# A graph layer's edge kernel: one-hots against PSUM constants, the node picked on VectorE, last edges found in blocks

## The chip, the cores and the metric

The kernel runs on one core of a Trainium2 chip. The core has five engines with queues of their own: TensorE (PE in the profile, its weight loads PEld), VectorE (DVE), ScalarE (ACT), GpSimd (POOL) and SyncE (SP, which here only issues DMAs). Each runs its instructions in the order in which they stand, and engines wait for each other by semaphores. The metric is the device time of one execution in microseconds.

## The reference

A graph with 12,500 nodes of 32 features and 400,000 edges, sorted by the node they end in (dst). Nodes are normalised and clipped, each edge gets a two-layer perceptron of its source row, its end's row and its own 32 features, and each node takes the largest result of its edges:

```python
h = jnp.maximum(_layernorm(x, axis=-1), 0.0)
rol, col = src, dst                              # edges, sorted by dst
e_feat = jnp.concatenate([h[rol], h[col], edge_attr], axis=-1)
hid = jax.nn.relu(e_feat @ W1 + b1)              # 96 -> 64
v = hid @ W2 + b2                                # 64 -> 32
x_cand = jax.ops.segment_max(v, col, num_segments=num_nodes)
return x + jnp.maximum(x_cand, h)
```

## The kernel before

**Layout.** The edges are cut into four stripes (NS = 4) that lie on four groups of 32 partitions, and each stripe into 196 chunks of C = 512 edges. Edges are handled a chunk at a time (2,048 edges over all stripes), two chunks c and c+1 per turn of the main loop, 98 turns in all. Node p * 98 + t lies in partition p, column t. Those 98 columns are also read as 7 groups (A1) of 14 (A0).

**Where a source row comes from.** A chunk needs 16 blocks of 128 source rows. Twelve of them are fetched by GpSimd with indirect DMAs from the copy of h in DRAM (`gather`, L148: one instruction per block of 128 rows, three to a buffer, 24 buffers). The other four (MM = 4) are made by TensorE, in what the code calls a tile (`tile(c, m)`, L344 to L359): h stands in SBUF as two float32r parts (`hs`, the rounded value and the rest), a one-hot over (partition, group) picks for each of 128 edges the group of 14 nodes that holds its source, and 7 groups x 2 parts = 14 matmuls with the one-hot as weights and `hs` as moving data (L356) add up to a 128 x 448 result: 14 candidate nodes x 32 features per edge. A matmul in front of these (L353) adds -1e30 to all candidates but one: its weights are `its`, a bfloat16 one-hot of the edge's place within its group, its moving data the constant table `others`. So a maximum over the 14 (L359, VectorE, out of PSUM) is the node's row.

**One-hots.** They are made by VectorE, chunk by chunk: seven tensor_scalar compares of the key row `kb` (float16, broadcast to all partitions by DMA) with the partition's own number (L340), and an eighth for `its` (L342). `kb` holds two rows per chunk, key and place.

**A turn of the loop** (L476 to L533), with a = c + 2 and b = c + 3, is written out by hand, and each engine keeps that order. GpSimd gathers for a and b. TensorE: tile (a,0); the first layer's source part (L444 with ht); tiles (a,1) and (a,2); the first layer's edge part for a and b (L444 with ea); the second layer for c and c+1 (L506) into two `pv` buffers, which are the same two that the tiles use; the first layer's end part (L444 with of and qw); the one-before-last chunk's reduction (L430); tile (a,3); transposes (L420); tile (b,0); L430; tile (b,1); L420; tiles (b,2) and (b,3). VectorE takes each tile's maximum, turns gathered rows into features with 32 x 32 transposes (`to_features`, L400 and L403), makes the one-hots of b and a + 2, scans each chunk along its edges (L513, a running maximum that restarts at each new node), adds the bias (L422) and makes `last` (L410), which marks each node's last edge within a window of 32 nodes, from `at`. ScalarE applies the first layer's relu (L491), makes the end's one-hot `of` with a square and a relu (L386, L387) and copies out results (L434), which SP writes to two tables `top_d` with one DMA per stripe. SP also loads ea and the window rows qw; db, pb and kb are issued from ScalarE's queue.

**Before the loop** x is normalised (VectorE for three of the four pieces, GpSimd for the piece with index GP = 3, L171 to L207), h is written to DRAM (L207), keys are computed and written, a penalty `pen` per edge is made from dst (L233, L234), h is split into its two parts (L241, L242) and q = h W1 for the end's part is computed (L249 to L267). Then a stage of its own (L271 to L303) loads all of dst, the next dst and the windows' limits and computes `at`, 196 chunks x 4 stripes at once, and a flag `general` that says whether the input breaks the assumptions of the fast path. These stages and the loop use pools that take over each other's memory, so a later one starts when the earlier one is done with it.

**After the loop** the two tables are read back (L546, L547) and merged (L549); h is put together again by GpSimd as the sum of its two parts (L541); maximum with h, sum with x, and out (L627 to L629).

The functions that the change touches follow with their line numbers.

Of the kernel before, what the change touches and what calls it, by code (L numbers as in the profile page):

```python
# [46 lines left out]
AHEAD = 4  # L47
PIECE = 2 * A0
GP = 3
ROUND = 12582912.0  # L50
LOW = 1e30
ZERO = 784
# [9 lines left out]
def gnn_kernel(ctx, tc, x, src, src_mm, src_t, dst, dst_next, dst_ext, lo, lo_c, hi, edge_attr, weights, w1, w2, b2, out):  # L62
# [19 lines left out]

# [9 lines left out]
    key_d = dram.tile([2, len(MMC) * MM * P], F16, name="key_d")  # L92
# [7 lines left out]
    for k, r in enumerate(pieces):  # L100
        (nc.sync, nc.scalar)[k % 2].dma_start(xs[:, r], x_v[:, r])
# [7 lines left out]
    iota_w = const.tile([P, W], F32, name="iota_w")  # L109
    nc.gpsimd.iota(iota_w, pattern=[[1, W]], base=0, channel_multiplier=0,  # L110
                   allow_small_or_imprecise_dtypes=True)
    below = const.tile([P, NCH], F32, name="below")
    for s in range(NS):
# [3 lines left out]
    place = const.tile([P, 1], F32, name="place")  # L117
    nc.gpsimd.iota(place, pattern=[[0, 1]], base=0, channel_multiplier=1,
                   allow_small_or_imprecise_dtypes=True)
    key_p = const.tile([P, A1], F32, name="key_p")  # L120
    nc.gpsimd.iota(key_p, pattern=[[1, A1]], base=0, channel_multiplier=A1,
                   allow_small_or_imprecise_dtypes=True)
    hs = const.tile([P, 2, A1, D, A0], F32R, name="hs")
    others = const.tile([P, D, A0], BF16, name="others")
# [13 lines left out]
    at = const.tile([P, NS, TS], F32, name="at")  # L138
# [14 lines left out]

    with tc.tile_pool(name="nodes", bufs=1) as pool, tc.tile_pool(name="nodes_ps", bufs=2, space=PSUM) as ps:
        zero = pool.tile([P, ZERO], F32, name="zero")
# [3 lines left out]
        sts = [pool.tile([P, 2, PIECE], F32, name=f"st{k}") for k in range(len(pieces))]  # L159
        shares = [(nc.vector, st, r) for st, r in zip(sts, pieces)]  # L160
        shares.append((nc.gpsimd, *shares.pop(GP)[1:]))
# [3 lines left out]
        iota_a = pool.tile([P, D, A0], F32, name="iota_a")  # L165
        nc.gpsimd.iota(iota_a, pattern=[[0, D], [1, A0]], base=0, channel_multiplier=0,
                       allow_small_or_imprecise_dtypes=True)
        lo_w = pool.tile([P, NCH], I32, name="lo_w")
        nc.scalar.dma_start(lo_w, ap(lo, 0, [[NCH, NS], [0, W], [1, NCH]]))

# [12 lines left out]
        with tc.manual_schedule(engines={DVE, SP}):  # L183
            for v, st, r in shares:
                n = r.stop - r.start
                total(v, st[:, 0, :n], xs[:, r])
                mean = st[:, 0, :n, None].to_broadcast([P, n, D])
                if v is nc.vector:
                    v.scalar_tensor_tensor(h[:, r], mean, -1.0 / D, xs[:, r], op0=ALU.mult, op1=ALU.add)
                else:  # L190
                    v.tensor_scalar(st[:, 0, :n], st[:, 0, :n], 1.0 / D, None, op0=ALU.mult)
                    v.tensor_tensor(h[:, r], xs[:, r], mean, op=ALU.subtract)
                nc.scalar.activation(sq[:, r], h[:, r], AF.Square)
            for v, st, r in shares:
                n = r.stop - r.start
                total(v, st[:, 1, :n], sq[:, r])
                nc.scalar.activation(st[:, 0, :n], st[:, 1, :n], AF.Sqrt, scale=1.0 / D, bias=eps)
            for v, st, r in shares:
                n = r.stop - r.start
                nc.vector.reciprocal(st[:, 1, :n], st[:, 0, :n])  # L200
                factor = st[:, 1, :n, None].to_broadcast([P, n, D])
                if v is nc.vector:
                    v.scalar_tensor_tensor(h[:, r], h[:, r], 0.0, factor, op0=ALU.max, op1=ALU.mult)
                else:
                    v.tensor_scalar(h[:, r], h[:, r], 0.0, None, op0=ALU.max)
                    v.tensor_tensor(h[:, r], h[:, r], factor, op=ALU.mult)
                nc.sync.dma_start(h_v[:, r], h[:, r])  # L207


            def group(out, of):  # L210
                nc.vector.tensor_scalar(out, of, 1.0 / A0, 0.5 / A0 - 0.5, op0=ALU.mult, op1=ALU.add)
                nc.vector.tensor_scalar(out, out, ROUND, None, op0=ALU.add)
                nc.vector.tensor_scalar(out, out, ROUND, None, op0=ALU.subtract)

            sp = pool.tile([P, len(MMC) * MM], I32, name="sp")
            nc.sync.dma_start(sp, src_mm)
            key = pool.tile([P, len(MMC) * MM], F32, name="key")
            group(key, sp)
            key16 = pool.tile([P, 2, len(MMC) * MM], F16, name="key16")
            nc.vector.tensor_copy(key16[:, 0], key)  # L220
            nc.vector.scalar_tensor_tensor(key16[:, 1], key, -float(A0), sp, op0=ALU.mult, op1=ALU.add)
            nc.sync.dma_start(key_d.rearrange("k (p e) -> p k e", p=P), key16)

            nc.vector.tensor_scalar(others, iota_a, place, -LOW, op0=ALU.not_equal, op1=ALU.mult)
            nc.vector.tensor_tensor(below, below, lo_w, op=ALU.subtract)


            de = pool.tile([P, EP // P + 1], I32, name="de")
            nc.sync.dma_start(de, ap(dst_ext, 0, [[EP // P, P], [1, EP // P + 1]]))
            pen = pool.tile([P, EP // P], BF16, name="pen")  # L230
            for k in range(0, EP // P, EP // P // 4):
                r = slice(k, k + EP // P // 4)
                nc.vector.tensor_tensor(pen[:, r], de[:, k + 1:k + 1 + EP // P // 4], de[:, r], op=ALU.not_equal)  # L233
                nc.vector.tensor_scalar(pen[:, r], pen[:, r], -LOW, None, op0=ALU.mult)  # L234
            nc.sync.dma_start(pen_d.rearrange("(p e) -> p e", p=P), pen)

        for r in pieces:
            g = slice(r.start // A0, r.stop // A0)
            h1, h2 = (hs[:, k, g].rearrange("p g f a -> p g a f") for k in range(2))
            hr = h[:, r].rearrange("p (g a) f -> p g a f", a=A0)  # L240
            nc.scalar.activation(h1, hr, AF.Copy)  # L241
            nc.vector.tensor_tensor(h2, hr, h1, op=ALU.subtract)  # L242

        for t in top_d:
            nc.scalar.dma_start(ap(t, 0, [[NT * D, P], [ZERO, NT * D // ZERO], [1, ZERO]]),
                                zero[:, None, :].to_broadcast([P, NT * D // ZERO, ZERO]))


        q_v = q_d.rearrange("(p t) o -> p t o", p=P)  # L249
        qs = pool.tile([P, NT, HID], F32, name="qs")  # L250
        for t in range(0, NT, 16):
            fours = [(k, min(4, NT - k)) for k in range(t, min(t + 16, NT), 4)]
            rows = fours[0][1] * D
            hp = ps.tile([P, 4, P], F32, name="hp")
            for i, (k, n) in enumerate(fours):
                nc.tensor.transpose(hp[:n * D, i], h[:, k:k + n].rearrange("p t f -> p (t f)"), ident)
            ht = pool.tile([P, 4, P], F32, name="ht", bufs=2)
            nc.vector.tensor_copy(ht[:rows, :len(fours)], hp[:rows, :len(fours)])
            for i in range(0, len(fours), 2):
                two = fours[i:i + 2]  # L260
                pp = ps.tile([P, 8, HID], F32, name="pp", bufs=4)
                for j, (k, n) in enumerate(two):
                    nc.tensor.matmul(pp[:, 4 * j:4 * j + n].rearrange("p t o -> p (t o)"), ht[:n * D, i + j],
                                     wq[:n * D, :n * HID], start=True, stop=True)
                k, n = two[0][0], sum(n for _, n in two)
                nc.scalar.activation(qs[:, k:k + n], pp[:, :n], AF.Copy)
        nc.sync.dma_start(q_v, qs)  # L267

    with tc.tile_pool(name="windows", bufs=1) as pool, tc.tile_pool(name="windows_ps", bufs=1, space=PSUM) as ps:  # L271
        lo_b = pool.tile([P, NS, NCH], I32, name="lo_b")
        hi_b = pool.tile([P, NS, NCH], I32, name="hi_b")
        nc.scalar.dma_start(lo_b, ap(lo, 0, [[0, P], [NCH, NS], [1, NCH]]))
        nc.scalar.dma_start(hi_b, ap(hi, 0, [[0, P], [NCH, NS], [1, NCH]]))
        di = pool.tile([P, NS, TS], I32, name="di")
        dn = pool.tile([P, NS, TS], I32, name="dn")
        nc.scalar.dma_start(di.rearrange("p s t -> p (s t)"), dst)
        nc.scalar.dma_start(dn.rearrange("p s t -> p (s t)"), dst_next)
        bad = pool.tile([P, 4, NS], F32, name="bad")  # L280
        step = pool.tile([P, TS], F32, name="step")
        wide = pool.tile([P, NCH], F32, name="wide")
        for s in range(NS):

# [22 lines left out]
    with tc.tile_pool(name="edges", bufs=3) as pool, tc.tile_pool(name="edges_ps", bufs=1, space=PSUM) as ps, \  # L307
# [8 lines left out]
        nc.vector.tensor_copy(iota_ps, iota_w)  # L316
        mm_rows = {}
        gh = {}
        hts = {}

        def load_keys(c):

# [369 lines left out]
```

## Time and profile before

| | us |
|---|---|
| median of 3 runs | 3158.97 (3158.54 to 3159.71) |
| the profiled execution, timed | 3161.57 |
| its span, first to last instruction | 3159.8 |
| TensorE busy | 3038.9 |
| GpSimd busy | 2331.2 |
| VectorE busy | 1822.4 |
| ScalarE busy | 562.8 |
| first gather starts | 31.05 |
| first tile's first matmul | 95.99 |
| last gather starts | 3059.8 |
| mean granted TensorE clock | 0.983 of full speed |

A row of the profile names the line, the engine, the operation, the tiles as out<-in, the count, the time busy in all and the mean of one, and then the idle time of the engine in front of it with what ended it. Matmuls overlap one another, so that the busy time of one is longer than the distance from one to the next. In a timeline the first two columns are start and duration in us, and idle time stands in brackets. GpSimd's busy time holds the issuing of a gather, not its transfer.

### The profile page before, as it was taken

To read this page: it belongs to the slowest core of one execution; us is meant where nothing else is said; L and a number is where in the kernel's file an instruction comes from. 1 tells how busy PE (TensorE), PEld (TensorE's weight loads), DVE (VectorE), ACT (ScalarE), POOL (GpSimd) and SP (SyncE) were. 2 spreads that over 40 slices of the span, in tenths; PEclk is the share of its full clock that TensorE was granted. 3 is DMA by queue.
4 is the path that set the end of the run, shared out by engine and by line. 5 is a ranking of instruction groups with operands and counts; after the bars stand their busy time and mean duration, and the time that the engine had idled before them with its cause. 6 is when DMAs were issued, how large, how long until landed. Compare 5 with 4: busy or idle time off the path is not lost. (4 is left out here: it accounts for less than half of the span.)

```text
span 3159.8 us, 59504 instructions
## 1 busy us (share of the span) xinstructions
PE 3038.9 (96%) x21969; PEld 2382.0 (75%) x21969; DVE 1822.4 (58%) x3999; ACT 562.8 (18%) x1007; POOL 2331.2 (74%) x2377
## 2 busy tenths in 40 slices
PE   2799999999999999999999999999999999999995
PEld 1578787777778777777778777777778777777873
DVE  6455555555555555555555555555555555555554
ACT  2121212112121212112121211112121211212121
POOL 7777777777777777777777777777777777777751
PEclk7899999999999999999999999999999999999997
DMA  6323332332333233233323332332333233233321
GB/s 246 109 64 74 90 73 63 90 80 68 72 89 76 64 84 83 71 69 89 78 64 77 88 72 63 90 83 64 73 89 76 64 87 85 66 72 88 78 57 63
DMA packets 203030, 255.38 MB, mean 81 GB/s; under 512 B 116062, under 2 KB 154862, under 8 KB 189551
## 3 DMA queue, kind: packets, MB, share of 16 engines
q10 hardware_dynamic: 42364, 138.10, 14.0%
q1 hardware_dynamic: 85330, 74.88, 10.1%
q0 software_dynamic: 75040, 38.57, 8.8%
q8 instruction: 173, 2.83, 0.4%
q14 instruction: 123, 1.00, 0.1%
HBM read 237.24 MB, written 14.05 MB: 80 GB/s over the span
## 5 line engine op out<-in xcount | busy, mean ns | idle before, releaser
L148 POOL DMA_INDIRECT gh<-h_d,src_i x2345 | 2301.2, 981 | 731.3 <-issue 567.8
L356 PE MATMUL pv<-hs,hot 128*128 128x448 f32 x10920 | 2435.0, 376 | 0.0
L356 PEld LDWEIGHTS pv<-hs,hot 128*128 128x128 f32 x10920 | 2058.5, 189 | 150.2 <-issue 0.3
L359 DVE TENSOR_REDUCE gm<-pv 128x32 f32<-128x448 f32 x780 | 486.3, 623 | 1149.9 <-PE pv L356 1147.7
L340 DVE TENSOR_SCALAR hot<-kb,key_p 128x512 fp32r<-128x512 f16 x1365 | 584.0, 487 | 6.1 <-DMA kb<-key_d 6.1
L491 ACT ACTIVATE hid<-ph,wt 128x512 f32<-128x512 f32 x392 | 237.2, 688 | 1325.7 <-PE ph L444 1312.2
L513 DVE TENSOR_TENSOR_SCAN sm<-pb,sm,pv 128x512 f32<-128x512 bf16 x195 | 249.6, 1280 | 133.4 <-PE pv L506 122.8
L353 PE MATMUL pv<-others,its 128*128 128x448 bf16 x780 | 281.3, 361 | 17.3 <-DMA qw<-q_d 10.6
L434 ACT ACTIVATE wo<-tr 128x64 f32<-128x64 f32 x196 | 43.7, 223 | 1146.6 <-PE tr L430 1056.4
L400 DVE STREAM_TRANSPOSE ht<-gh 128x96 f32<-128x96 f32 x782 | 209.5, 268 | 0.0
L353 PEld LDWEIGHTS <-its 128*128 128x128 bf16 x780 | 74.9, 96 | 172.4 <-issue 151.8
L430 PEld LDWEIGHTS tr<-so,last 128*64 128x64 f32 x3136 | 108.0, 138 | 112.6 <-issue 107.0
L386 ACT ACTIVATE of<-db,below 128x512 f32<-128x512 int32 x196 | 141.4, 721 | 64.5 <-DMA db<-in_dst_ext 64.5
L387 ACT ACTIVATE of<-of,ones 128x512 f32<-128x512 f32 x196 | 142.3, 726 | 6.4
L430 PE MATMUL tr<-so,last 128*64 128x64 f32 x3136 | 135.2, 229 | 3.3 <-DVE so L422 3.3
L410 DVE TENSOR_TENSOR last<-iota_ps,at 128x512 f32<-128x512 f32 x196 | 132.8, 678 | 0.0
L422 DVE TENSOR_TENSOR so<-tr,wt 128x512 f32<-128x512 f32 x196 | 127.9, 653 | 3.0 <-PE tr L420 3.0
L420 PE MATMUL tr<-ident,sm 128*128 128x128 f32 x784 | 117.8, 272 | 1.5 <-DVE sm L513 0.8
L444 PE MATMUL ph<-ht,wt 32*64 32x512 f32 x1568 | 111.3, 617 | 0.0
L420 PEld LDWEIGHTS tr<-ident,sm 128*128 128x128 f32 x784 | 97.4, 141 | 16.7 <-ACT wo L434 2.0
L506 PE MATMUL pv<-hid,wt 64*32 64x512 f32 x1568 | 109.3, 605 | 0.7 <-ACT hid L491 0.7
L444 PE MATMUL ph<-ea,wt 32*64 32x512 f32 x1568 | 109.1, 613 | 0.0
(78 smaller groups left out, 478.4 us busy)
## 6 DMA issues: line engine op xcount, KB each, us to landing
ea<-in_edge_attr SPq DMA_DIRECT2D x49, 1024.0 KB
db<-in_dst_ext ACTq DMA_DIRECT2D x49, 1024.0 KB
kb<-key_d ACTq DMA_DIRECT2D x97, 512.0 KB
gh<-h_d,src_i POOLq DMA_INDIRECT x2345
pb<-pen_d ACTq DMA_DIRECT2D x49, 512.0 KB
qw<-q_d SPq DMA_DIRECT2D x784, 8.0 KB
top_d<-wo SPq DMA_DIRECT2D x784, 4.0 KB
top_d<-zero ACTq DMA_DIRECT2D x2, 1568.0 KB
```

The costliest lines, as they stand in the source:

```text
L148: nc.gpsimd.indirect_dma_start(out=parts[-1][:, i, :], out_offset=None, in_=h_d[:, :], in_offset=bass.IndirectOffsetOnAxis(ap=src_i[:, c, ...
L340: nc.vector.tensor_scalar(hot[:, k], keys[c][:, 0], key_p[:, k:k + 1], None, op0=ALU.is_equal)
L353: nc.tensor.matmul(po, its[:, e], others.rearrange("p f a -> p (f a)"), start=True, stop=False)
L356: nc.tensor.matmul(po, hot[:, k, e], hs[:, part, k].rearrange("p f a -> p (f a)"), start=False, stop=(k == A1 - 1 and part == 1))
L359: nc.vector.tensor_reduce(rows, po.rearrange("p (f a) -> p f a", a=A0), axis=AX.X, op=ALU.max)
L387: nc.scalar.activation(of, of, AF.Relu, bias=ones, scale=-1.0)
L400: nc.vector.transpose(ht[:, r].rearrange("p k e -> p (k e)"), gh[c][part][:, :r.stop - r.start].rearrange("p k f -> p (k f)"))
L420: nc.tensor.transpose(px[:, j, :], sm[:, j * P:(j + 1) * P], ident)
L430: nc.tensor.matmul(pw[g * 2 * W:(g + 1) * 2 * W], last[:, j, 2 * g:2 * g + 2].rearrange("p s w -> p (s w)"), so[:, j, g * 2 * D:(g + 1) * ...
L444: nc.tensor.matmul(ph[s][x * HID:(x + 1) * HID], w[g], e[g], start=start, stop=stop)
L491: nc.scalar.activation(hid[s], ph[s], AF.Relu, bias=b1c)
L513: nc.vector.tensor_tensor_scan(sm, loaded.pop(c + x)[2], pv[x], before, op0=ALU.add, op1=ALU.max)
```

## The change

It has five parts.

1. **The pick.** `its`, `others` and the matmul L353 go; `key_d` and `kb` hold one row per chunk. `tile` multiplies the 128 x 448 result with a mask of the edge's place in its group (`mask_of`, made once per chunk for four tiles) and takes the maximum of the product, which is the node's row since h is not negative. The places are computed on the chip from `src_i` (`places`), for 16 chunks ahead of the loop and for the rest in one turn of it.
2. **The one-hots.** The constants that are compared with (`counts`: places in a window, key numbers, places in a group) lie in PSUM. Five of the seven groups are made by VectorE with two tensor_tensor compares (2 and 3 groups), two by ScalarE with a square and a relu each.
3. **Last edges.** `at` is computed in 14 blocks of 14 chunks, each loaded by four DMAs on ScalarE's queue one turn ahead and computed between two tiles (`load_block`, `make_block`); the stage in front of the loop goes. The flag is put together after the loop.
4. **Memory and order at the start.** What the tiles need has a pool of its own (`early`, `early_ps`) that is there from the start, so that the tiles of chunks 0 and 1 stand among the node stages; the order of all engines but GpSimd is written out by hand from there on. GpSimd's part of the normalisation is shorter: the last product of its piece is VectorE's. The penalty's scaling is ScalarE's, the zero fills of `top_d` are issued by SP.
5. **h at the end** is summed by GpSimd right behind its last gather, into the memory of `src_i`.

```diff
-            for k in groups:
-                nc.vector.tensor_scalar(hot[:, k], keys[c][:, 0], key_p[:, k:k + 1], None, op0=ALU.is_equal)
-            if A1 - 1 in groups:
-                nc.vector.tensor_scalar(its, keys.pop(c)[:, 1], place, None, op0=ALU.is_equal)
+    consts = early_ps.tile([P, C], F32, name="consts")[:, :W + A1 + A0]
+    count_ps, key_ps, place_ps = consts[:, :W], consts[:, W:W + A1], consts[:, W + A1:]
+    nc.vector.tensor_copy(consts, counts)
...
+    def one_hots(c, start, stop):
...
+        nc.vector.tensor_tensor(hot_of(c)[:, start:stop], keys[c][:, None, :].to_broadcast([P, n, MM * P]),
+                                key_ps[:, start:stop, None].to_broadcast([P, n, MM * P]), op=ALU.is_equal)
+    def one_hots_act(c, groups=BY_ACT):
...
+            nc.scalar.activation(away, keys[c], AF.Square, bias=key_n[:, k:k + 1])
+            nc.scalar.activation(hot_of(c)[:, k], away, AF.Relu, bias=ones, scale=-1.0)
+    def mask_of(c):
...
+            nc.vector.tensor_tensor(
+                masks[c], place_ps[:, None, :].to_broadcast([P, MM, A0]),
+                place_k[:, (c - MMC.start) * MM:(c - MMC.start + 1) * MM, None].to_broadcast([P, MM, A0]),
+                op=ALU.is_equal)
```

```diff
-            nc.tensor.matmul(po, its[:, e], others.rearrange("p f a -> p (f a)"), start=True, stop=False)
             for k in range(A1):
                 for part in range(2):
                     nc.tensor.matmul(po, hot[:, k, e], hs[:, part, k].rearrange("p f a -> p (f a)"),
-                                     start=False, stop=(k == A1 - 1 and part == 1))
-            nc.vector.tensor_reduce(rows, po.rearrange("p (f a) -> p f a", a=A0), axis=AX.X, op=ALU.max)
+                                 start=(k == 0 and part == 0), stop=(k == A1 - 1 and part == 1))
+        of_group = po.rearrange("p (f a) -> p f a", a=A0)
+        one = early.tile([P, D, A0], F32, name="one", bufs=2)
+        nc.vector.tensor_tensor(one, of_group, masks[c][:, m, None, :].to_broadcast([P, D, A0]), op=ALU.mult)
+        nc.vector.tensor_reduce(mm_rows[c][:, m, :], one, axis=AX.X, op=ALU.max)
```

```diff
+    def make_block(b):
+        di, dn, lo_b, hi_b = loaded_b.pop(b)
+        at = ats[b] = early.tile([P, NS * BLOCK, J], F32, name="at")
...
+        nc.vector.tensor_tensor(at, di, lo_b[:, :, None].to_broadcast([P, NS * BLOCK, J]), op=ALU.subtract)
+        nc.vector.tensor_tensor(step, di, dn, op=ALU.is_gt)
+        nc.vector.tensor_reduce(bad[:, b, 0:1], step, axis=AX.XY, op=ALU.max)
+        nc.vector.tensor_tensor(step, di, dn, op=ALU.not_equal)
+        nc.vector.scalar_tensor_tensor(at, at, 1.0, step, op0=ALU.add, op1=ALU.mult)
+        nc.vector.tensor_tensor(wide, hi_b, lo_b, op=ALU.subtract)
+        nc.vector.tensor_reduce(bad[:, b, 1:2], wide, axis=AX.X, op=ALU.max)
```

The loop's turn with its new calls, and the end:

```diff
+            if (c + 6) % BLOCK == 0 and (c + 6) // BLOCK < NB:
+                load_block((c + 6) // BLOCK)
+            if a == NCH - 2:
+                nc.gpsimd.tensor_tensor(again.rearrange("p (g a) f -> p g a f", a=A0),
+                                        hs[:, 0].rearrange("p g f a -> p g a f"),
+                                        hs[:, 1].rearrange("p g f a -> p g a f"), op=ALU.add)
             tile(a, 0)
...
-            one_hots(b, range(3))
+            one_hots_act(b)
+            one_hots(b, 0, 2)
             tile(a, 1)
             to_features(a, 1)
-            one_hots(b, range(3, A1))
+            one_hots(b, 2, BY_ACT.start)
+            mask_of(b)
             last = [lasts(c)]
...
             tile(a, 3)
+            one_hots_act(a + 2)
...
-            one_hots(a + 2, range(4))
+            one_hots(a + 2, 0, 2)
...
-            one_hots(a + 2, range(4, A1))
+            one_hots(a + 2, 2, BY_ACT.start)
+            mask_of(a + 2)
             tile(b, 2)
             to_features(b, 2)
+            if c == 2 * AHEAD:
+                places(FIRST, len(MMC))
+            if (c + 4) % BLOCK == 0 and (c + 4) // BLOCK < NB:
+                make_block((c + 4) // BLOCK)
             tile(b, 3)
...
-        h = pool.tile([P, NT, D], F32, name="h_again")
-        nc.gpsimd.tensor_tensor(h.rearrange("p (g a) f -> p g a f", a=A0),
```

## The prediction

> **What bounds the kernel now.** I read the page's busy shares first, then the groups by shape, then the timeline of one turn of the loop (two chunks, c and c+1), and last the end of the span.
>
> ```profile
> PE 3038.9 (96%) x21969; PEld 2382.0 (75%) x21969; DVE 1822.4 (58%) x3999; ACT 562.8 (18%) x1007; POOL 2331.2 (74%) x2377
> ...
> L148 POOL DMA_INDIRECT gh<-h_d,src_i x2345 | 2301.2, 981 | 731.3 <-issue 567.8 <-DMA gh<-h_d,src_i 104.6 <-DVE ht L400 17.8
> L340 DVE TENSOR_SCALAR hot<-kb,key_p 128x512 fp32r<-128x512 f16 x1365 | 584.0, 487 | 6.1 <-DMA kb<-key_d 6.1
> L359 DVE TENSOR_REDUCE gm<-pv 128x32 f32<-128x448 f32 x780 | 486.3, 623 | 1149.9 <-PE pv L356 1147.7 <-issue 2.2
> L353 PE MATMUL pv<-others,its 128*128 128x448 bf16 x780 | 281.3, 361 | 17.3 <-DMA qw<-q_d 10.6 <-DVE its L342 6.3 <-DVE sm L513 0.3
> L410 DVE TENSOR_TENSOR last<-iota_ps,at 128x512 f32<-128x512 f32 x196 | 132.8, 678 | 0.0
> ```
>
> TensorE is busy 96% and VectorE idles waiting for it, so TensorE sets the pace. But GpSimd's 74% hides a second bound: its 731 us of idle time are 2,345 pieces of some 0.30 us in front of each gather, so that it runs without a pause from 31 us to 3061 us. The timeline shows both paces:
>
> ```profile
> 1509.99 0.94 POOL L148 DMA_INDIRECT gh<-h_d,src_i  x1 [0.30 <-issue]
> ...
> 1511.04 1.63 DVE L340 TENSOR_SCALAR hot<-kb,key_p 128x512 fp32r<-128x512 f16 x4
> 1511.24 1.15 POOL L148 DMA_INDIRECT gh<-h_d,src_i  x1 [0.30 <-issue]
> 1512.70 0.94 POOL L148 DMA_INDIRECT gh<-h_d,src_i  x1 [0.30 <-DVE hot L340]
> ...
> 1517.33 0.10 PEld L353 LDWEIGHTS <-its 128*128 128x128 bf16 x1 [0.21 <-issue]
> ...
> 1520.34 0.10 PEld L353 LDWEIGHTS <-its 128*128 128x128 bf16 x1 [0.21 <-issue]
> ...
> 1523.51 1.11 PE L444 MATMUL ph<-ht,wt 32*64 32x512 f32 x16
> ```
>
> Tile follows tile after 3.01 us (1517.33 to 1520.34). The turn repeats after 30.86 us: its L444 ht matmuls at 1523.51 stand at 1492.65 in the turn before. An undisturbed gather takes 0.94 + 0.30 = 1.248 us; one beside L340 takes 1.15 to 1.18. Counted over the trace from 200 to 3000 us: the 667 gathers that lie beside L340 or L342 are 116 ns longer on average, the 1,076 that lie beside only L410, L422, L359 or L513 (all with a PSUM operand) are not longer at all. 24 gathers a turn at the mean of 1.290 us are 30.96 us, undisturbed 29.96. So the bounds lie 0.1 us apart, and a gain on TensorE is worth what GpSimd lets through.
>
> **The change, part by part.**
>
> *The matmul with `others` goes* (L353, one of 15 in each tile). Its 361 ns overlap their neighbours; what a tile loses is the difference between 3.01 us and 14 matmuls that start 0.200 us apart (read from the starts inside a tile) = 2.80 us: 0.21 us, 1.7 us for the 8 tiles of a turn. TensorE's turn: 30.86 - 1.7 = 29.15 us. If the 0.21 us in front of a tile is a gap that stays, the saving still is one slot of 0.20.
>
> *VectorE picks the node*: before, one reduce out of PSUM per tile (623 ns); now a product PSUM x mask and a reduce out of SBUF. No row has this product. Bounds: 0.57 us (L359's 623 less its start-up) and 0.68 (L410, more elements); I take 0.65 and 0.57, since a dependent pair does not overlap, so +0.65 us per tile, 5.2 us a turn.
>
> *One-hots*: 7 L340 at 0.41 to 0.49 us and L342 (0.35) per chunk go from VectorE; five groups come back as two products with a PSUM operand (1,024 and 1,536 elements). L410 has 512 in 0.678, so bounds are n x 0.678 (1.36, 2.03) and its per-element rate with one start-up (1.2, 1.75); I take the latter, as both L359 and the 784-element rows show about 0.15 us of start-up. With the mask (56 elements, some 0.15) it is 3.1 us in place of 3.4. VectorE's turn comes to some 22.5 us of 30: under both others, but it now comes late at one place (next part). Two groups go to ScalarE: Square and Relu at 0.72 each, 2.9 us a chunk; its turn grows from 5.6 to 11.4 us. The pair for b stands behind hid and window_hots and ends 9 us after L444's ht matmuls, needed 14 us after; wo queues behind the pair for a+2 and stays ahead of the next transposes. I cost that at nothing; without that cover each late wo would hold `tr` and TensorE by up to 1 us.
>
> *The wait that arises.* Both edge accumulators `pv` use the two buffers of the tiles. Count from the start of tile (a,2): product of (a,1) 0.2-0.86, reduce 1.4, transpose 1.6, one-hots (2,5) 3.25, mask 3.4, lasts 3.95, product of (a,2) 4.6. TensorE has done the tile (2.8) and L444's ea (3.85) and then waits for that buffer: 0.85 us. Queued behind it on TensorE are the second-layer matmuls (L506), the windows and the next tile, and VectorE's scans wait for those; all else keeps its slack. TensorE's turn then is 29.15 + 0.85 = 30.0 (29.2 if the product overlaps, 30.6 at the upper bounds of one-hots and product).
>
> *GpSimd* loses the disturbance: 24 x 1.248 = 29.96 a turn. What still disturbs it are operations with two SBUF inputs:
>
> ```profile
> 70.48 0.97 DVE L290 TENSOR_TENSOR step<-di,dn 128x784 f32<-128x784 int32 x1
> 70.56 1.71 POOL L148 DMA_INDIRECT gh<-h_d,src_i  x1 [0.30 <-issue]
> 71.48 0.97 DVE L291 SCALAR_TENSOR_TENSOR at<-at,step 128x784 f32<-128x784 f32 x1
> ```
>
> From 65.44 to 87.71 us 14 gathers took 22.3 us in place of 17.5, 4.8 us more beside 16.5 us of such operations: 0.29 us per us. make_block has 1.7 us of them (L293: 196 elements in 0.36), 14 times; the start has some 16 us (second halves, pen, key, places). Together 40 us x 0.29 = 12 us, bounds 0 and 40.
>
> The Trainium skill, page "SBUF — State Buffer", section on the two separate sides, says that the pair of ports shared by VectorE and GpSimd is locked for a whole instruction and the loser is blocked fully. Here a gather beside 1.63 us of L340 grew by 0.21 us only, so the trace shows a partial delay; by the page the blocks would cost all of the 40 us, which would put the end some 28 us later.
>
> *The start.* GpSimd's 5.56 us product (L206) and its clamp go to VectorE as one operation, so h_d is complete after about 22 us in place of 28.2 and the first gather starts at 25.5 instead of 31.05 (a late second x piece could make it 27). The windows stage (59 to 87 us on VectorE) leaves the front: `di`, `dn` and the limits come in 14 blocks by four ACT-queue issues each (0.4 us, ahead of kb's use by a turn). VectorE, by the rows of these operations, has h until 22, then key (1.9), seven copies (4.0) and four second halves (5.9), then the first one-hots (2.7): tile (0,0) starts at about 38 us in place of 96. But SP now issues the two zero fills, pen_d and then ea, db and pb in a row; pen ends on ScalarE at about 43, what is in front lands by 48, and db landed 21 us after its issue (86.5 to 107.5). So window_hots of the first pair comes at about 70 and chunk 2's first tile at about 75 (70 to 85) in place of 131.96.
>
> *The end.*
>
> ```profile
> 3112.48 0.38 DVE L400 STREAM_TRANSPOSE ht<-gh 128x96 f32<-128x96 f32 x2
> ...
> 3134.14 11.29 POOL L541 TENSOR_TENSOR h_again<-hs 128x3136 f32<-128x3136 f32 x1 [73.45 <-DMA top_d<-wo]
> 3139.11 9.80 DVE L549 TENSOR_TENSOR acc<-acc,part 128x896 f32<-128x896 f32 x4 [11.39 <-DMA part<-top_d]
> ```
>
> h_again moves behind the last gather, 40 us from the end. L549 then costs what L627 costs for the same shapes, 3 x 1.09 + 0.62 = 3.9 in place of 9.8: 5.9 us off the end (0 at worst, if the pieces' loads come apart). From the last transpose of gathered rows (3112.9) to 3159.8 are 46.9 us, then 41. The few operations for `general` lie under the top_d writes (3129 to 3133.7).
>
> *The sums.* By gathers: 25.5 + 2345 x 1.248 (2927) + 12 + 2 for landing (an estimate from the 2.9 us between the end of L206 and the first gather, which hold one landing) + 41 = 3007 us. By TensorE: 75 + (3159.8 - 131.96) - 97 turns x (30.86 - 30.0) - 5.9 = 3013 us. They are all but tied, and two paces this near cost a little of each other's slack: I take 3016 for the span. The profiled span of 3159.8 (the run itself 3161.57) stands 0.8 us over the median of 3158.97, so the time is 3015.
>
> **Rivals.** *The new wait is larger*: product, one-hots and waits at their upper ends give a turn of 30.6: 75 + 3027.8 - 25 - 5.9 = 3072 us. For it speaks that VectorE's chain from pv to pv has no slack; against it that ScalarE's share could not lengthen it. *The gathers stay disturbed*, the PSUM constants do not free them: 25.5 + 2345 x 1.290 + 2 + 41 = 3094. Against it stand the 1,076 undelayed gathers beside PSUM readers. *VectorE becomes the bound and the kernel slower*: it decides from a turn of 31.6 us on. If broadcast products with a PSUM operand cost twice L410's rate, VectorE gains 5.5 + 5.3 us, 33.3 us a turn: 75 + 3027.8 + 97 x 2.4 - 5.9 = 3330. L410 broadcasts both of its inputs, one of them out of PSUM, and shows none of it. *The pick is free*: no wait at pv and little disturbance, gathers alone, 2998.
>
> **How the numbers follow.** Forecast (3000 to 3035) 0.64; larger wait 0.22; gathers still disturbed 0.05; pick free 0.05; slower 0.03; the rest lands near no change. 3158.97 has 0.2% = 6.3 us as what a measurement can tell: faster 0.96, within 0.01, slower 0.03. The range of 8 in 10 takes the tie from below (2996) and most of the larger wait (3062).
>
> **What would show it.** A mean gather near 948 ns (not 981), 24 of them in about 30.0 us; a wait of the second-layer matmuls for VectorE of 0.5 to 1.2 us a turn; tiles 2.80 us apart; VectorE's transposes waiting for gathered rows in places; the first gather near 25 us, the last near 2965. Wrong would be a turn over 30.4 us, gathers still at 980 ns, or a VectorE without idle time.

## The result and the profile after

The changed kernel takes 3175.86 us (median of five runs, 3173.08 to 3178.64), the kernel before 3158.97 (five runs, 3158.54 to 3163.22): a ratio of 1.0051, 95% interval 1.0036 to 1.0065. It is slower by half a percent where 3015 us was forecast. The profiled execution has a span of 3174.9 us.

The rows of the page that answer to those shown of before (busy time and share, then groups: count, busy time, mean ns of one, idle time in front):

```profile
PE 3028.0 (95%) x21189; PEld 2341.0 (74%) x21189; DVE 2250.2 (71%) x3869; ACT 1089.7 (34%) x1795; POOL 2256.2 (71%) x2376
...
L154 POOL DMA_INDIRECT gh<-h_d,src_i x2345 | 2235.2, 953 | 798.9 <-issue 564.5
...
L242 DVE TENSOR_TENSOR one<-pv,mask 128x448 f32<-128x448 f32 x780 | 483.8, 620 | 721.5 <-PE pv L238 718.0
L557 ACT ACTIVATE hid<-ph,wt 128x512 f32<-128x512 f32 x392 | 237.3, 688 | 1352.4 <-PE ph L506 1098.3
L207 DVE TENSOR_TENSOR hot<-kb,consts 128x1536 fp32r<-128x1536 f16 (+2 forms) x388 | 565.8, 1458 | 0.0
L243 DVE TENSOR_REDUCE gm<-one 128x32 f32<-128x448 f32 x780 | 484.0, 621 | 26.9
```

Most of this is as forecast: the gathers' mean falls from 981 to 953 ns, the product costs 620 ns and its reduce 621, VectorE is at 71% and still waits for TensorE. So the sum of engine costs doesn't explain the loss. The distances between the turns do. Taking each turn's first relu of `hid` (L557), 97 distances: an ordinary one is 30.35 us (30.86 before), the first is 40.08, and seven, every 14 turns, are 46.36, 44.36, 43.97, 42.92, 44.93, 41.84 and 46.67 us. Together the seven are 98.6 us over the ordinary turn; the turns right behind them are 0.9 us shorter each, which leaves 92 us.

ScalarE's timeline through one of them (start, duration, engine, line; ACTq is the issuing of DMAs from ScalarE's queue):

```profile
657.21 0.33 ACTq L192 DMA_DIRECT2D kb<-key_d  x1
657.58 0.55 ACTq L450 DMA_DIRECT2D db<-in_dst_ext  x1
658.23 0.52 ACTq L451 DMA_DIRECT2D pb<-pen_d  x1
660.46 0.60 ACTq L269 DMA_DIRECT2D di<-in_dst  x1
661.11 15.72 ACTq L269 DMA_DIRECT2D dn<-in_dst_next  x1
676.86 6.35 ACTq L273 DMA_DIRECT2D lo_b<-in_lo  x1
683.25 0.98 ACTq L273 DMA_DIRECT2D hi_b<-in_hi  x1
684.27 2.42 ACT L557 ACTIVATE hid<-ph,wt 128x512 f32<-128x512 f32 x4 [26.90 <-issue]
```

And TensorE's, in the same stretch:

```profile
669.12 1.11 PE L506 MATMUL ph<-ht,wt 32*64 32x512 f32 x16
670.16 6.00 PE L238 MATMUL pv<-hs,hot 128*128 128x448 f32 x28
685.01 3.70 PE L506 MATMUL ph<-ea,wt 32*64 32x512 f32 x16 [8.86 <-ACT hid L557]
688.65 1.96 PE L574 MATMUL pv<-hid,wt 64*32 64x512 f32 x16
690.53 2.01 PE L506 MATMUL ph<-of,qw 32*64 32x512 f32 x16
```

The relu could start when L506's ht matmuls end (670.2). It starts at 684.27, because it stands on ScalarE behind four DMA issues of `load_block`, of which two took 22 us. TensorE does its next two tiles and then waits 8.86 us.

The wait is not the whole loss. The seven waits of TensorE are 6.3 to 11.2 us long, 62.6 in all. Within each of them the granted TensorE clock falls to 0.5 and stays there for 10 to 17 us (here from 680.6 to 694.3), and what TensorE does behind the wait is slower: L506's ea matmuls take 3.70 us and those of `of` 2.01, where an ordinary turn has 1.11 for each. Between 131 and 3039 us the clock is below full speed at these seven places only, and in e1_front and e1_shift_2 below, which have no such waits, nowhere in that stretch. So some 30 of the 92 us are not waiting but this slower work.

The odd blocks (1, 3 and so on to 13) are loaded in a turn that also loads `ea`, `db` and `pb`; there dn's issue takes 9.9 to 17.9 us and lo_b's 5.8 to 8.8. In the turns of the even blocks each takes 0.6 us (once 1.2). By the packets that the trace has of this queue, dn's issue ends when 82 to 91% of db's 128 rows are through, and lo_b's when 45 to 74% of pb's are, in all seven. SP's issues are not held meanwhile: three or four of them fall into each of dn's, none over 0.43 us. One of them:

```profile
665.80 0.42 SPq L447 DMA_DIRECT2D ea<-in_edge_attr  x1
```

The wait forecast at `pv` is there too, on TensorE's weight loads for the second layer:

```profile
1522.75 0.13 PEld L574 LDWEIGHTS pv<-hid,wt 64*32 64x32 f32 x2 [0.81 <-DVE hot L207]
1523.37 0.18 PEld L574 LDWEIGHTS pv<-hid,wt 64*32 64x32 f32 x14 [0.48 <-DVE one L242]
```

The first load of the group goes at once (the 0.81 us in front of it pass while L506's matmuls run); the second stands idle for 0.48 us until VectorE's product of tile (a,2) has ended. The second layer takes 1.70 us from start to end in place of 1.09, so the wait costs 0.61 us a turn.

### The profile page after: what moved, and what is told of

Read it like the earlier page. It is cut to its first block, busy times and chain, and to the rows that moved or that the text cites. A ratio compares the mean times of both kernels' runs of the same rounds, so it can differ in the third digit from the quotient of the medians.

```text
span 3174.9 us, 58841 instructions
## 1 busy us (share of the span) xinstructions
PE 3028.0 (95%) x21189; PEld 2341.0 (74%) x21189; DVE 2250.2 (71%) x3869; ACT 1089.7 (34%) x1795; POOL 2256.2 (71%) x2376
## 5 line engine op out<-in xcount | busy, mean ns | idle before, releaser
L154 POOL DMA_INDIRECT gh<-h_d,src_i x2345 | 2235.2, 953 | 798.9 <-issue 564.5
L238 PE MATMUL pv<-hs,hot 128*128 128x448 f32 x10920 | 2359.4, 371 | 1.6 <-DVE hot L207 1.0
L242 DVE TENSOR_TENSOR one<-pv,mask 128x448 f32<-128x448 f32 x780 | 483.8, 620 | 721.5 <-PE pv L238 718.0
L557 ACT ACTIVATE hid<-ph,wt 128x512 f32<-128x512 f32 x392 | 237.3, 688 | 1352.4 <-PE ph L506 1098.3
L207 DVE TENSOR_TENSOR hot<-kb,consts 128x1536 fp32r<-128x1536 f16 (+2 forms) x388 | 565.8, 1458 | 0.0
L243 DVE TENSOR_REDUCE gm<-one 128x32 f32<-128x448 f32 x780 | 484.0, 621 | 26.9
L217 ACT ACTIVATE hot<-away,ones 128x512 fp32r<-128x512 f32 x392 | 283.8, 724 | 239.3 <-issue 229.6
L216 ACT ACTIVATE away<-kb,key_n 128x512 f32<-128x512 f16 x392 | 277.9, 709 | 0.0
L506 PE MATMUL ph<-ea,wt 32*64 32x512 f32 x1568 | 127.3, 646 | 62.6 <-ACT hid L557 62.6
L574 PE MATMUL pv<-hid,wt 64*32 64x512 f32 x1568 | 170.1, 638 | 0.7 <-ACT hid L557 0.7
L506 PE MATMUL ph<-of,qw 32*64 32x512 f32 x1568 | 121.6, 651 | 22.3 <-DMA qw<-q_d 22.3
L474 DVE TENSOR_TENSOR last<-consts,at 128x512 f32<-128x512 f32 x196 | 132.1, 674 | 0.0
```

The source lines that it names most:

```text
L154: nc.gpsimd.indirect_dma_start(out=parts[-1][:, i, :], out_offset=None, in_=h_d[:, :], in_offset=bass.IndirectOffsetOnAxis(ap=src_i[:, c, ...
L207: nc.vector.tensor_tensor(hot_of(c)[:, start:stop], keys[c][:, None, :].to_broadcast([P, n, MM * P]), key_ps[:, start:stop, None].to_broad ...
L216: nc.scalar.activation(away, keys[c], AF.Square, bias=key_n[:, k:k + 1])
L217: nc.scalar.activation(hot_of(c)[:, k], away, AF.Relu, bias=ones, scale=-1.0)
L238: nc.tensor.matmul(po, hot[:, k, e], hs[:, part, k].rearrange("p f a -> p (f a)"), start=(k == 0 and part == 0), stop=(k == A1 - 1 and par ...
L242: nc.vector.tensor_tensor(one, of_group, masks[c][:, m, None, :].to_broadcast([P, D, A0]), op=ALU.mult)
```

## The experiments

Twelve kernels ran, four on each of three chips, and the kernel before beside them on each. On the second chip the kernel before took 3161.0 us (seven runs); on the first and third it took 4035.8 and 4126.7, and the records show a granted TensorE clock of 0.88 to 0.91 in the mean. Times from those two chips are compared only within a chip; what is read from them is in the rows.

**1. What holds ScalarE** (first chip). Two theories stood for the long issue: a wait for a semaphore that an earlier DMA shares (A), and the queue itself (B).

`e1_mid`, the block's loads issued inside `load`, between pb and the qw loads:

```diff
+                if block is not None:
+                    load_block(block)
                 for k in range(c, min(c + LOAD, NCH)):
...
-                load(k)
-            if (c + 6) % BLOCK == 0 and (c + 6) // BLOCK < NB:
-                load_block((c + 6) // BLOCK)
+                load(k, block=block)
```

> The block's four loads (di, dn, lo_b, hi_b) are issued from ScalarE's queue in the same turns as in the changed kernel and still behind db and pb, but in the program's order they stand in front of the eight qw loads, no longer behind them. Theory A (an issue of ScalarE's is held until the DMA eight places earlier in the program's order, SP's counted too, has landed; there it is a qw that SP itself issues late, behind db's landing): at most two of the seven turns of 42 to 47 us are left, every dn and lo_b issue under 7 us, time 3176 - 93 = 3083 us (3070 to 3095). Theory B (the issue stands behind the 1.5 MB of db and pb in its own queue, or in the memory traffic): seven long turns as before, 3165 to 3185 us.

Measured: 4211.2 us (1.0436 of before, 1.0409 to 1.0462). Seven turns of 51.7 to 54.0 us in a median of 41.4 stay, as B has it. One of them:

```profile
1487.33 0.55 ACTq L450 DMA_DIRECT2D db<-in_dst_ext  x1
1487.97 0.52 ACTq L451 DMA_DIRECT2D pb<-pen_d  x1
1490.80 0.61 ACTq L269 DMA_DIRECT2D di<-in_dst  x1
1491.45 15.13 ACTq L269 DMA_DIRECT2D dn<-in_dst_next  x1
1506.62 5.83 ACTq L273 DMA_DIRECT2D lo_b<-in_lo  x1
```

No qw load stands in front of dn any more, and its issue takes 15.13 us all the same. A falls.

`e1_shift`, no block's loads in a turn that loads ea, db and pb, and `e1_double`, all of them in such a turn (`- 8 + 2 * (nb % 2)` in place of the last term):

```diff
-            if (c + 6) % BLOCK == 0 and (c + 6) // BLOCK < NB:
-                load_block((c + 6) // BLOCK)
+            for nb in range(1, NB):
+                if c == nb * BLOCK - 6 - 2 * (nb % 2):
+                    load_block(nb)
```

> The loads of an odd block come one turn earlier, so that no block's loads fall into a turn that also loads ea, db and pb. Theories A and B: no turn over 33 us between the first and the last, the idle time in front of hid on ScalarE falls by some 95 us, time 3083 us (3070 to 3095). Theory C (the long turns are not made by the loads but by make_block on VectorE, one turn later): the long turns stay, 3165 to 3185 us.

> The loads of an even block come one turn earlier, so that all 13 blocks' loads fall into a turn that loads ea, db and pb. A and B: 13 long turns in place of seven, 3176 + 6 x 13.3 = 3256 us (3235 to 3275). C: 3176 us.

Measured: e1_shift 4188.7 us (1.0381, 1.0358 to 1.0404), e1_double 4238.4 (one run). In e1_shift every dn and lo_b issue of the loop takes 0.62 to 0.64 us; in e1_double all 13 dn issues take 13.6 to 17.6 and there are 13 turns of 51 to 55 us. The issues do what A and B say. The times do not: e1_shift still has turns of up to 46.7 us, and 13 long turns cost 50 us more than none, not 13 x 13, since the turn behind each is 5 to 11 us shorter on this chip, where TensorE is slowed anyway. So the price still had to be measured on a chip where TensorE is not slowed.

**2. The price, and what holds the issue: the queue or the traffic** (second chip, the kernel before at 3161.0 us).

`e1_front`, the block's loads in the turns of the changed kernel but ahead of db and pb:

```diff
+            if (c + 6) % BLOCK == 0 and (c + 6) // BLOCK < NB:
+                load_block((c + 6) // BLOCK)
             for k in range(c + AHEAD, min(c + AHEAD + 2, NCH)):
                 load(k)
-            if (c + 6) % BLOCK == 0 and (c + 6) // BLOCK < NB:
-                load_block((c + 6) // BLOCK)
```

> The block's four loads stay in the turns of the changed kernel and on ScalarE's queue, but stand in front of db and pb there, not behind them. Theory A has fallen (with the qw loads behind them the seven long turns stayed, dn's issue still 14 to 17 us). Theory B1 (dn's and lo_b's issue is held while the queue works off the 1.5 MB of db and pb ahead of it): every dn and lo_b issue under 1 us, no turn over 34 us on a chip where the kernel before takes 3159 us, time 3083 us (3070 to 3095) there. Theory B2 (the traffic of such a turn, 2.5 MB, holds any issue): dn's issues stay at 14 to 17 us, 3175 us.

Measured: 3083.7 us (0.9756, 0.9740 to 0.9772). The same loads, in the same turn, on the same queue:

```profile
643.32 0.33 ACTq L192 DMA_DIRECT2D kb<-key_d  x1
643.69 0.59 ACTq L269 DMA_DIRECT2D di<-in_dst  x1
644.32 0.64 ACTq L269 DMA_DIRECT2D dn<-in_dst_next  x1
645.00 0.62 ACTq L273 DMA_DIRECT2D lo_b<-in_lo  x1
645.66 0.52 ACTq L273 DMA_DIRECT2D hi_b<-in_hi  x1
647.27 0.59 ACTq L450 DMA_DIRECT2D db<-in_dst_ext  x1
```

In all 13 blocks dn's issue takes 0.57 to 0.85 us. B2 (the traffic) falls, B1 stands: what counts is what lies ahead in ScalarE's queue, here db and pb, 1.5 MB. Whether their bytes, their rows or their number count was not tried. Except for the first and the last, no turn is over 31.05 us.

`e1_shift_2`, the kernel of e1_shift on this chip:

> The kernel of e1_shift again, since the chip of the first four runs granted TensorE a clock of 0.88 and took 4036 us for the kernel before, so that the long turns hid behind TensorE there. On a chip where the kernel before takes 3159 us: 3083 us (3070 to 3095), every turn between the first and the last under 34 us.

Measured: 3085.0 us (0.9761, 0.9745 to 0.9777), the longest turn between first and last 31.05 us. Two different cures, one time: the seven long turns cost 3175.9 - 3084 = 92 us (the changed kernel's 3175.9 is from the runs of the result, where the kernel before took 3159.0, 2 us less than here). C falls with it; make_block still runs once in 14 chunks, and its turns have 30.4 to 30.5 us.

**3. The pick: its wait at pv and its matmul.** `e3_order` is e1_shift with one call moved:

```diff
             to_features(a, 1)
-            one_hots(b, 2, BY_ACT.start)
             mask_of(b)
...
                 sms.append(sm)
+            one_hots(b, 2, BY_ACT.start)
             tile(a, 3)
```

> e1_shift with VectorE's one-hots of b's groups 2 to 4 moved from in front of tile (a,2)'s product to behind the scans. Theory D (what holds the second-layer matmuls 0.6 us a turn is VectorE's chain from product to product): the wait in front of the second-layer matmuls falls under 0.2 us; the turn goes from 30.3 to the gathers' 24 x 1.256 = 30.15 us, 10 to 20 us under e1_shift_2, some 3068 us. Rival E (gathers are no floor): TensorE's 29.7 us, 60 us under. Rival F (the one-hots now hold the product of tile (a,3) and with it tile (b,0)): no gain, up to 30 us over.

Measured: 3062.7 us (0.9684, 0.9667 to 0.9701), 22 under e1_shift_2. The wait is gone:

```profile
1036.88 1.11 PE L506 MATMUL ph<-ea,wt 32*64 32x512 f32 x16
1037.93 1.09 PE L574 MATMUL pv<-hid,wt 64*32 64x512 f32 x16
1038.94 1.11 PE L506 MATMUL ph<-of,qw 32*64 32x512 f32 x16
```

The turn is 29.74 us for the first half. Then TensorE has caught up with the gathers, and every other turn grows to 30 to 34 us with VectorE waiting for gathered rows; the mean of all is 30.15. D holds in kind (22 us where it had 10 to 20), E's turn of 29.7 us is there for the first half only, and F falls.

`e2_noprod` and, on the third chip, `e2_noprod_2` leave the product out (the reduce takes `of_group`, so that the row is the maximum over the 14 nodes):

> e1_shift with the product left out: the reduce reads the 14 candidates from PSUM unmasked, so that a source row made by TensorE is the maximum over its group of 14 nodes. VectorE does 8 x 0.62 = 5 us less a turn. Theory D (the wait of the second-layer matmuls for the buffer that VectorE holds, 0.6 us a turn, is the product's, and gathers are next at 24 x 1.256 = 30.15 us): 10 to 20 us under e1_shift, some 3068 us, the wait in front of the second-layer matmuls under 0.2 us. Rival E (gathers are no floor): TensorE's 29.7 us, 60 us under e1_shift. Rival F (the wait costs nothing, tiles alone set the turn): as e1_shift within 5 us.

> The kernel of e2_noprod again (e1_shift without the product: the reduce takes the 14 candidates from PSUM unmasked), for a chip where the kernel before takes 3159 us. Theory D: the wait in front of the second-layer matmuls gone, turn 29.74 us as in e3_order until the gathers are caught up with, 20 to 25 us under e1_shift_2, some 3062 us. F: 3085 us.

Measured: 4061.7 us beside 4188.7 for e1_shift, and 4207.3 us (1.0204 of before) on the third chip; neither answers to a forecast for a chip that is not slowed (the 127 us under e1_shift are more than D, E or F had). But the last two full turns, behind the last gather, run undisturbed on the slowed chips too: 30.33 and 30.35 us in e1_shift, 29.74 and 29.68 in both of these. So the 0.6 us wait is the product's place in VectorE's chain, whether the product goes or something else in the chain does.

`e2_extra`, e3_order with a matmul of L353's size back in front of each tile:

```diff
+        nc.tensor.matmul(po, its, others, start=True, stop=False)
         for k in range(A1):
```

> e3_order with a bfloat16 matmul of the size of L353's put back in front of each tile (both operands zero, so that it adds nothing): TensorE's side of the pick is undone, VectorE's stays. Theory I (in the trace of before L353 starts 0.04 us ahead of the tile's first L356 matmul, and the gap in front of a tile stays without it, so that it was worth some 0.08 to 0.12 us a tile): the turn goes from e3_order's 29.74 to 30.4 to 30.7 us, time 3062 + 97 x (0.25 to 0.55), as the gathers hide the first 0.4 us: 3085 to 3115 us. Rival J (0.21 us a tile, as the prediction had it): turn 31.4 us, 3190 us.

Measured: 4236.4 us (1.0286, 1.0259 to 1.0314, third chip). Its last two full turns are 31.12 us each, in place of 29.7: 1.4 us, 0.18 a tile. That is between I (0.08 to 0.12) and J (0.21), nearer to J. A run of tiles in it:

```profile
4116.23 0.36 PE L240 MATMUL pv<-others,its 128*128 128x448 bf16 x1
4116.27 3.20 PE L243 MATMUL pv<-hs,hot 128*128 128x448 f32 x14
4119.31 0.37 PE L240 MATMUL pv<-others,its 128*128 128x448 bf16 x1
4119.35 3.20 PE L243 MATMUL pv<-hs,hot 128*128 128x448 f32 x14
```

From tile to tile are 3.08 us, where three tiles in a row of e3_order take 8.84 us, some 2.95 each.

**4. The start.** `e4_start` is e3_order with the zero fills of top_d issued behind the first loads of the edges and four buffers for q's staging:

```diff
-            qs = pool.tile([P, 16, HID], F32, name="qs", bufs=2)
+            qs = pool.tile([P, 16, HID], F32, name="qs", bufs=4)
...
         for c in range(AHEAD):
             load(c, nc.sync)
+        for t in top_d:
+            nc.sync.dma_start(ap(t, 0, [[NT * D, P], [ZERO, NT * D // ZERO], [1, ZERO]]),
+                              zero[:, None, :].to_broadcast([P, NT * D // ZERO, ZERO]))
```

> e3_order with a changed start: the two zero fills of top_d (3.1 MB) are issued behind the first loads of ea, db, pb and qw, and q's staging has four buffers for two. Theory G (the first pair waits for db, which lands 20 us after its issue behind the fills, and for q_d, which waits for its buffers): the first relu of the loop starts at 85 to 92 us in place of 98.8, the first turn takes 31 to 35 us in place of 40, in all 10 to 20 us under e3_order. Rival H (the gathers' start sets the pace): no gain.

Measured: 3058.1 us (0.9679, 0.9663 to 0.9695), 4.6 under e3_order, with ranges that overlap. The start moved by more than that. The waits of the first pair, first in the changed kernel:

```profile
82.30 0.72 ACT L468 ACTIVATE of<-db,below 128x512 f32<-128x512 int32 x1 [24.14 <-DMA db<-in_dst_ext]
87.85 4.92 PE L506 MATMUL ph<-of,qw 32*64 32x512 f32 x16 [16.47 <-DMA qw<-q_d]
```

and in e4_start:

```profile
65.58 0.72 ACT L464 ACTIVATE of<-db,below 128x512 f32<-128x512 int32 x1 [15.79 <-DMA db<-in_dst_ext]
71.05 2.97 PE L502 MATMUL ph<-of,qw 32*64 32x512 f32 x14 [7.85 <-DMA qw<-q_d]
```

The first relu starts at 83.5 us in place of 96.4, and TensorE's turn is 29.36 us. But TensorE then meets the gathers after 20 turns, not after 50, and the mean turn is 30.20: H is mostly right. The first gather starts at 22.9, the last at 3004.4, the end is at 3052.5; they are the bound now.

**5. What frees the gathers.** `e2_sbuf` is e4_start with one operand in another memory:

```diff
-                                key_ps[:, start:stop, None].to_broadcast([P, n, MM * P]), op=ALU.is_equal)
+                                counts[:, W + start:W + stop, None].to_broadcast([P, n, MM * P]), op=ALU.is_equal)
```

> e4_start with the one-hots' group numbers read from SBUF instead of PSUM, nothing else. Theory K (a VectorE operation with two SBUF inputs delays the gathers beside it, as L340 and L342 did before, 116 ns each; one with a PSUM input does not): gathers beside the one-hots go from 0.952 to some 1.07 us, the mean of all from 0.954 to 0.98 to 1.00, time 3058 + 2345 x 0.026 to 0.046 = 3120 to 3165 us. Rival L (what delayed them was L340's form, a tensor_scalar, not where its inputs lie): 3058 us within 6.

Measured: 4070.8 us (0.9889, 0.9844 to 0.9935, third chip, where gathers wait for free buffers and the time says nothing on K). The gathers' mean goes to 1038 ns (953.9 in e4_start, 954.0 in e1_sp and 954.1 in e2_extra on this same chip), 196 us in all; L falls, and K was too small by far. VectorE's one-hot and the gathers around it:

```profile
1996.18 0.95 POOL L154 DMA_INDIRECT gh<-h_d,src_i  x1 [0.30 <-issue]
1996.78 1.73 DVE L207 TENSOR_TENSOR hot<-kb,counts 128x1536 fp32r<-128x1536 f16 x1
1997.43 1.91 POOL L154 DMA_INDIRECT gh<-h_d,src_i  x1 [0.31 <-issue]
```

A gather begun before the operation is not longer (0.95). One begun in it ends 0.83 us after the operation's end (1998.51 to 1999.34). Over the 361 gathers begun in a one-hot, 0.83 us is the median, and nearly all lie within 0.01 of it. With the operand in PSUM (e4_start), 447 gathers begun in a one-hot take 0.952 us in the median, as alone.

**6. Another queue.** `e1_sp`, the changed kernel with `load_block(..., nc.sync)` in the loop:

> The changed kernel with the block's four loads issued by SP, behind ea and the qw loads of that turn, in place of ScalarE. B1: ScalarE's issues of db and pb stay short, hid is never held by an issue, no long turns; SP's dn issue may be held behind ea's 1 MB, which only delays the qw and top_d of that turn, used two turns later: 3083 us (3075 to 3100). Against it (the block's loads late on SP would hold make_block, one turn later, and with it VectorE): some turns over 34 us, 3100 to 3175 us.

Measured: 4241.5 us (1.0292, 1.0269 to 1.0316, third chip). No issue of the block's loads takes over 1.0 us on SP, none of ScalarE's is long, and the 51 to 55 us turns at every 14th place are not there. That agrees with B1, but it doesn't show what a large load ahead of them on SP would do: by the packets of SP's queue, ea's last row was through 6 to 34 us before di's issue in all 13 turns, as the qw loads stand between and wait. The time can't be set beside e1_shift, which did not run on this chip.

## Why the prediction was wrong

The step that failed is one sentence of the start: the blocks come "by four ACT-queue issues each (0.4 us, ahead of kb's use by a turn)", costed at nothing. It took an issue's price from issues that had no large load in front of them (di and dn of the kernel before, 0.45 and 0.46 us), and named kb as the only thing that could be late. Behind db and pb, dn's and lo_b's issues cost ScalarE 20 to 24 us (19 in one), and what was late is `hid`, next in ScalarE's order, and then TensorE, whose clock was halved on top. With the loads ahead of db and pb, or in another turn, the 92 us are gone. The terms, by the first relu of the loop, the 97 turns and the end:

| term | forecast | measured | difference, us |
|---|---|---|---|
| seven turns with long issues | 0 | 92 net | +92 |
| ordinary turn, 97 times | 30.0 | 30.35 | +34 |
| first relu (chunk 2's first tile) | 79.2 (75) | 98.8 (92.7) | +20 |
| first turn over an ordinary one | 0 | 9.7 | +10 |
| end, from the last turn's relu | 37.1 | 40.4 | +3 |

(79.2 is the forecast tile plus before's 4.2 us from tile to relu.) On 3013, the sum by TensorE, these make 3172, with 3174.9 measured. Without the first row the change would have been faster: 3084 us.

- *The matmul with `others`*: 1.7 us a turn was forecast. TensorE's turn free of waits went from 30.86 to 29.74, 1.1 us; putting the matmul back costs 1.4 (in e2_extra the other matmuls stand 0.205 us apart, in the kernel before 0.203, which is 0.24 us a turn). The forecast took a tile without it as 14 x 0.200 us. The matmuls stand 0.204 us apart in the changed kernel (0.203 before), and some 0.1 us more than one slot stays in front of a tile, so that it is 2.95 us long, not 2.80.
- *VectorE picks the node, the one-hots, the mask*: product 0.62 (0.65 forecast), reduce 0.62 (0.57), one-hots 1.18 and 1.72 (1.2 and 1.75), mask 0.20 (0.15). Right; VectorE is no bound. The 0.57 has no ground: it takes 0.05 us off L359 for a start-up that the part on the one-hots puts at 0.15, and the reduce out of SBUF takes as long as the one out of PSUM did (621 and 623 ns).
- *The wait that arises*: right in place and kind, 0.61 us for 0.85. With the term before, 30.86 - 1.12 + 0.61 is the 30.35 measured.
- *GpSimd loses the disturbance*: right in that, 981 to 953 ns. The reason given was wrong in one point: 0.21 us beside "1.63 us of L340" was read as a partial delay, but that row holds four operations, and the gather at 1511.24 ended 0.91 us after the first of them (1511.04 to 1511.48), though the other three ran beside it. Over all 410 gathers of before that begin within an L340 operation, the median end is 0.82 us after that operation's. So a gather is held for nearly all that is left of one operation. The Trainium skill, page "SBUF — State Buffer", section on the two separate sides, says so (a VectorE operation with two SBUF inputs that starts first has the shared ports to its end, against a GpSimd operation that reads SBUF). e2_sbuf agrees with it (0.83 us), and the prediction weighed it wrongly. The 12 us for what still disturbs came to some 3 (2235.2 us of gathers less 2345 x 0.952), as few gathers lie beside such operations.
- *A gather's own pace*: an undisturbed gather is 0.952 us long, not 0.944, and 1.256 from the next instead of 1.248: 19 us over all. In e4_start, where gathers are the bound, the mean distance is 1.272, so that "by gathers 3007" is 3052 there.
- *The start*: the first gather at 23.4 (25.5 forecast) is right. db landed 20 us after its issue, as taken, but was issued at 62 and not at 48: SP's own queue, with q's writes waiting for two staging buffers and then the fills, was not worked out. And qw, which waits for q_d, was later still.
- *The end*: 2.6 us gained for 5.9. `part`'s pieces come apart: the merge (L628 of the changed kernel) starts its first three at 3156.57, 3159.55 and 3161.53; that bound was given as possible.
- *Rivals*: "the new wait is larger" gave 3072 by a turn of 30.6. None of them had a DMA issue or the clock in it; the one on the slower side looked at VectorE alone, which has 29% to spare.

The Trainium skill, page "Perfetto Trace Analysis", section "DMA Instruction — HWDGE (DVE, Sync)", says that the profiled span of a DMA with descriptors made by hardware, as SP and ScalarE issue them, starts when its semaphores are satisfied and holds the making of its descriptors, not the transfer. The rows agree: a qw load that waits for db shows as idle time on SP with an issue of 0.32 us behind it, dn as an issue of 15.72.

## What to carry to other kernels

A DMA issued from a compute engine's queue has a price on that engine, and here it was set by what lay ahead of it in that queue: put small loads in front of large ones, or into another turn (92 us here for the place of two lines). A wait of TensorE can cost more than its length (92 us here for 62.6 of waiting): look at the granted clock behind it. When a step is moved into a loop, look at the turn it lands in, not at the average turn: 14 does not divide by 4, so that every other block met the large loads. And a gain on one engine ends where the next bound lies: of the 0.6 us a turn that e3_order freed, the gathers let through a third.

## What the runs showed of the hardware that was not expected

- Behind 1.5 MB in ScalarE's queue one small DMA was issued at once (di, 0.6 us) and the next held ScalarE 9.9 to 17.9 us, until 82 to 91% of the rows of db ahead of it were through. How much fits wasn't measured.
- Within each of seven waits of 6.3 to 11.2 us, the granted TensorE clock fell to 0.5, and stayed there 10 to 17 us.
- A gather begun during a VectorE operation with two SBUF inputs ends 0.83 us after that operation, whatever was left of it; with one of the inputs in PSUM it isn't delayed.
- The same 128x448 float32r matmuls start 0.2012 us apart in the mean in e4_start (mostly 0.200), 0.2030 in the kernel before and 0.2042 in e3_order. The edit from e3_order to e4_start touches none of them; as far as it tells, only places of tiles in SBUF change for them (`zero` goes into the pool of the one-hots). The difference of the means times 112 matmuls gives 0.34 of the 0.38 us between their turns. A gather's 0.944 us in the kernel before and 0.952 in the changed ones is another such shift. What makes either wasn't tried.
- On the first chip the same kernel e1_shift takes 4189 us instead of the second's 3085, and there it is 4% slower than the kernel before, not 2% faster. Stretches of it on the first chip (us, busy time of PE, PEld, DVE, ACT and POOL with counts, granted clock, DMA share, GB/s), a turn in the middle and one behind the last gather:

```profile
2000.00:2041.00 41.00, 35.37 (x215) 24.00 (x214) 21.40 (x39) 9.03 (x16) 22.23 (x24) 0.92 0.17 31
4096.00:4126.00 30.00, 30.00 (x224) 23.66 (x216) 21.99 (x38) 10.88 (x18) 0.00 (x0) 1.00 0.01 2
```

The same work takes 41 us with gathers beside it and 30 without, with a granted clock of 0.92 and 1.00. The clock alone would account for 3 of the 11 us of this turn; the rest stays open, and so does why the kernel before takes 4036 and 4127 us on the first and third chips.

The fastest kernel of the study is e4_start, 3058.1 us, 3.2% under the kernel before on the second chip; e1_front, which moves two lines of the change, is 2.4% under it.
